# Local attention with a convolution branch: where the softmax inverse is applied, and which engine does three of the conv taps

## The chip, the cores and the metric

One core of a Trainium2 chip. The time is device microseconds of one execution; several executions are measured and the median is given. A profile of one further execution gives every instruction with its engine, start and duration. The engines are TensorE (PE; its weight loads are listed apart as PEld), VectorE (DVE), ScalarE (ACT), GpSimd (POOL) and the queue that issues most transfers, SyncE (SP).

## The reference

Three layers in float32 on a tensor of 2 images, 256 channels, 48 by 48 pixels. Only the first is touched by the change; after it come a state-space layer and a mixture of eight experts.

The first layer normalises the image by groups of channels and then computes two things from the normalised image `x`:

```python
q = (c1x1(x, Wq, bq) * HD ** -0.5)            # 4 heads of 64 channels
k, v = c1x1(x, Wk, bk), c1x1(x, Wv, bv)
att = softmax(einsum(q, unfold7x7(k) + unfold7x7(pe)))   # 49 neighbours of each pixel, reflected edges
out_att = einsum(att, unfold7x7(v))
hid = relu(dwconv3x3(x, w1))                   # one filter per channel
oc = dwconv3x3(hid, w2)
wts = softmax(einsum(Wfc, x), over 9)          # oc is the same for the nine, so the weights add up to 1
return rate1 * out_att + rate2 * oc            # added to the layer's input
```

## The kernel before

The first layer, called layer 0 here, is a *flow*: every piece of work is declared as an operation with an engine, a cost in ns, the operations it needs, the buffers it takes and frees, and a due time. Before anything is built, a planner (`Flow.run`) plays the flow through with these costs and writes out a fixed order for each engine; each engine then runs its list strictly in that order and waits at every instruction for what it needs. Due times are a block's number times `PACE0`, shifted by a table `LEAD0` with one entry for each kind of operation. So a cost or a lead that is edited changes the order on all engines. The GpSimd list is in order as well (`on_pool`): compute and the issue of transfers share it.

**Attention.** Each image is cut into 18 blocks of 8 by 16 queries, 36 blocks in all. A block sees 14 by 22 = 308 keys. The 256 channels lie as two halves (`h`) of 128 partitions, with two heads (`j`) in each half. For a block and a half, the steps are:

- `score` (L776, PE): two matmuls with 64 rows each, into a PSUM pair `banks`;
- `least` (L786, DVE): adds the mask, takes the minimum, writes `prob`;
- `exps` (L797, ACT): two exponentials over 308 keys, with the sums into `den`;
- once for the block, after both halves: `rden` (L852, DVE), the reciprocal of the four sums;
- `divide` (L803, ACT): two multiplications of 128x308 by the reciprocal;
- `turn` (L810, PE): six transposes of `prob`, keys onto the partitions, in chunks of 110, 110 and 88 keys (`KCH`);
- `copy` (L818, L819, ACT): two copies out of PSUM into `pt`;
- `mix` (L828, PE): six matmuls with the values `val` into a PSUM `bank`;
- `add` (L835, DVE): adds the product and the bias `bv1` onto the image.

The matmuls of `score` use half of the array's rows and those of `mix` half of its columns; the planner books a switch between these modes. Keys (L665, added with a place term at L671 and mirrored at the edges by `kb`, small copies on GpSimd, L678 to L685; the place term itself is made at L654), queries (L621, scaled at L631 in three pieces) and values (L711) are matmuls of their own. Values go through HBM into a table, and each block loads its part (L860) on the SP queue.

**Convolution.** Channels and rows are cut into 8 strips (two images, two halves, two strips of 24 rows). The first conv writes `hid`: the centre tap on ACT (L557), six taps on DVE (L561, multiply and add), and taps 1 and 7 by `added`: ACT multiplies into a tile `ct` (L599, two buffers), and a transfer issued on GpSimd adds the tile onto `hid` in SBUF (L603). Then relu on ACT (L565), and the second conv adds all nine taps onto the image on DVE (L573).

PSUM has room for four `bank` and two `banks` (pairs). After layer 0 the state-space layer starts with transposes of the image (L988), which need its last `add`.

Of the kernel before, what the change touches and what calls it, by code (L numbers as in the profile page):

```python
# [37 lines left out]
P = 128  # L38
# [3 lines left out]
HD = 64  # L42
# [5 lines left out]
KCH = ((0, 5), (5, 5), (10, 4))  # L48
# [74 lines left out]
class Flow:  # L123
# [8 lines left out]
    def __init__(self, room, lead):  # L132

        self.room, self.lead, self.ops = dict(room), lead, {}
# [8 lines left out]
    @classmethod  # L143
    def kind(cls, key):
        return key if isinstance(key, str) else cls.kind(key[0])

# [3 lines left out]
    def rank(self):  # L150

        after = {k: [] for k in self.ops}
        for k, o in self.ops.items():
            for n in o["needs"]:
                after[n].append(k)
        tail, left = {}, {k: len(after[k]) for k in self.ops}
        ends = [k for k in self.ops if not left[k]]
        for k in ends:
            o = self.ops[k]
            same = [tail[a] for a in after[k] if self.ops[a]["due"] == o["due"]]  # L160
            tail[k] = self.span(o) + max(same, default=0) + self.HOP
            for n in o["needs"]:
                left[n] -= 1
                if not left[n]:
                    ends.append(n)
        return {k: o["due"] - tail[k] - self.lead.get(self.kind(k), 0) for k, o in self.ops.items()}, after
# [62 lines left out]
class Kernel:  # L229
# [49 lines left out]
    def begin_flow(self, pool, room, pace, lead):  # L279

        self.m, self.pace, self.flow, self.tiles, self.last = pool, pace, Flow(room, lead), {}, {}
# [52 lines left out]
    def layer0(self, ctx):  # L334
# [5 lines left out]
        room = dict(bank=4, banks=2, q=2, prob=3, pt=4, val=3, vout=2, hid=2, place=2, ct=2)  # L340
        self.begin_flow(self.pool("att", 1, ctx), room, self.PACE0, self.LEAD0)
        self.kp = [wts.tile([P, HP, HP], F32, name=f"kp{h}") for h in range(NH)]
        self.xp = {(b, h): wts.tile([P, H, W], F32, name=f"xp{b}{h}") for b in range(B) for h in range(NH)}
# [19 lines left out]
    def prepare(self, wts):  # L363
# [15 lines left out]
        for key, cost in (("cst", 9500), ("vec", 9000), ("wp", 8500), ("Wk", 9500), ("Wq", 10500), ("Wv", 11500),  # L379
                          ("win", 22000)):  # L380
            self.arrival((key, 0), cost)
# [7 lines left out]
            new("w2r", NH * 9), v["w2"], r["rate2"], None, ALU.mult), ("vec", 0))  # L389

        self.op(0, ("bv1", 0), "DVE", 220, lambda: vec.tensor_scalar(
            new("bv1", NH), v["bv"], r["rate1"], None, ALU.mult), ("vec", 0))
        self.op(0, ("wv1", 0), "POOL", 1600, lambda: nc.gpsimd.tensor_scalar(
            l0["Wv"], l0["Wv"], r["rate1"], None, ALU.mult), ("vec", 0), ("Wv", 0))
# [63 lines left out]
    def group_norm(self, b):  # L458
# [7 lines left out]
        for h in range(NH):  # L466
# [7 lines left out]
            for i in range(pieces):  # L474
                if i % 2 == 0:
                    self.arrival(("x", (b, h, i // 2)), (4500, 16000)[b] + (i // 2 * NH + h + 1) * 700)
# [50 lines left out]
    def convolutions(self, b):  # L527
# [16 lines left out]
        for n in range(NH * strips):  # L544
# [33 lines left out]
            for k in (1, 7):  # L578
                last = self.added(due, ("1", key, k), rows[0], partial(tap, rows, k=k), hidden, lambda h=h: (self.xp[b, h], 0),
                                  lambda w=w1, k=k: w[:, k : k + 1], before, last)  # L580
            for k in range(9):
                if k != 4 and k not in (1, 7):
# [4 lines left out]
            rest = taps  # L587
            for i, k in enumerate(rest):
                self.op(due, ("c2", (key, k)), "DVE", 1385, partial(mac2, k), *before, uses=[("hid", key)] if i == len(rest) - 1 else [])
                before = [("c2", (key, k))]  # L590

    def added(self, due, key, first, places, out, of, weight, before, last):
# [3 lines left out]
        def product():  # L596
            t = self.large_tile("ct", key, [P, CR + 1, W])
            dst, src = places(o=(t, first), i=of())
            nc.scalar.activation(dst, src, AF.Identity, scale=weight())  # L599

        def issue():
            (dst, _), (t, _) = (places(o=o, i=of()) for o in (out(), (T["ct", key], first)))
            nc.gpsimd.dma_start(dst.rearrange("p r c -> p (r c)"), t.rearrange("p r c -> p (r c)"), accum_op=ALU.add)  # L603

        self.op(due, ("cp", key), "ACT", 1220, product, *before, takes=[("ct", key)])
# [4 lines left out]
    def queries(self, b, rb):  # L610
# [4 lines left out]
        for h in range(NH):  # L615
# [10 lines left out]
            def scale(h=h, key=key):  # L626
                if h == 0:
                    self.large_tile("q", (b, rb), [P, NH, NCB, QR * QC])
                ps = T["bank", ("q", key)][:, : QR * W].rearrange("p (r c) -> p r c", r=QR)
                for cb in range(NCB):  # L630
                    nc.scalar.activation(  # L631
                        T["q", (b, rb)][:, h, cb, :].rearrange("p (r c) -> p r c", r=QR), ps[:, :, cb * QC : (cb + 1) * QC],
                        AF.Identity, bias=l0["bq8"][:, h : h + 1], scale=-(HD ** -0.5),
                    )
# [3 lines left out]
            self.op(c, ("q", key), "ACT", 870, scale, ("qp", key), ("bq8", 0), ("q", (b, rb, 0)) if h else None,  # L638
                    takes=[] if h else [("q", (b, rb))], uses=[("bank", ("q", key))])

    def keys(self, b, g):
# [17 lines left out]
        for h in range(NH):  # L659
# [16 lines left out]
            def border(kp=kp):  # L676
# [4 lines left out]
                for j in range(PAD):  # L681
# [8 lines left out]
                    *[("score", (i, h)) for i in range(old + 1) if b],  # L690
# [64 lines left out]
    def block(self, c):  # L755
# [11 lines left out]
        for h in range(NH):  # L767
            key = (c, h)

            def scores(h=h, key=key):  # L770
                if h == 0:
                    self.large_tile("prob", c, [P, 4, NKEY])
                ps = self.banks_for(("s", key))
                for j in range(2):
# [4 lines left out]
                    )  # L779

# [20 lines left out]
            def divide(h=h):  # L801
                for a in range(2 * h, 2 * h + 2):
                    nc.scalar.mul(T["prob", c][:, a, :], T["prob", c][:, a, :], T["rden", c][:, a : a + 1])  # L803


            def turn(h=h, key=key):
                ps = self.banks_for(("t", key))
                for i, (kr, nr) in enumerate(KCH):
                    for j in range(2):
                        nc.tensor.transpose(  # L810
                            ps[: nr * KC, j, i * P : (i + 1) * P], T["prob", c][:, 2 * h + j, kr * KC : (kr + nr) * KC],
                            self.ident
                        )

            def copy(h=h, key=key):
                full, short = KCH[0][1] * KC, KCH[-1][1] * KC
                pt, ps = self.large_tile("pt", key, [P, 2, len(KCH), P]), T["banks", ("t", key)]
                nc.scalar.copy(pt[:full, :, :2, :].rearrange("p j i q -> p j (i q)"), ps[:full, :, : 2 * P])  # L818
                nc.scalar.copy(pt[:short, :, 2, :], ps[:short, :, 2 * P : 3 * P])  # L819


            def mix(h=h, key=key):
                po = self.bank_for(("o", key))
                for i, (kr, nr) in enumerate(KCH):
                    nk = nr * KC
                    for j in range(2):
                        a = 2 * h + j
                        nc.tensor.matmul(  # L828
                            po[j * HD : (j + 1) * HD, :P], lhsT=T["val", c][:nk, i, a * HD : (a + 1) * HD],
                            rhs=T["pt", key][:nk, j, i, :], start=i == 0, stop=i == len(KCH) - 1,  # L830
                        )

            def add(h=h, key=key):
                x = self.x[b][:, h, :].rearrange("p (r c) -> p r c", r=H)[:, r0 : r0 + QR, c0 : c0 + QC]
                nc.vector.scalar_tensor_tensor(  # L835
                    x, T["bank", ("o", key)][:, :P].rearrange("p (r c) -> p r c", r=QR), self.l0["bv1"][:, h : h + 1],
                    x, ALU.add, ALU.add
                )

            self.op(c, ("score", key), "PE", 512, scores, ("q", (b, rb, h)), *[k for k in rows if k[1][2] == h],  # L840
                    ("score", (c, 0)) if h else None,
                    takes=[("banks", ("s", key))] + ([] if h else [("prob", c)]), mode="rows", uses=[("q", (b, rb))] if last and h == NH - 1 else [])
            self.op(c, ("least", key), "DVE", 950, least, ("score", key), ("cst", 0), ("least", (c, 0)) if h else None,
                    uses=[("banks", ("s", key))])
            self.op(c, ("exps", key), "ACT", 1170, exps, ("least", key), ("exps", (c, 0)) if h else None)
            self.op(c, ("divide", key), "ACT", 990, divide, ("rden", c))
            self.op(c, ("turn", key), "PE", 655, turn, ("divide", key), takes=[("banks", ("t", key))], uses=[("prob", c)])
            self.op(c, ("copy", key), "ACT", 870, copy, ("turn", key), takes=[("pt", key)], uses=[("banks", ("t", key))])
            self.op(c, ("mix", key), "PE", 660, mix, ("copy", key), ("val", c), takes=[("bank", ("o", key))], mode="tiled",
                    uses=[("pt", key)] + ([("val", c)] if h == NH - 1 else []))  # L850
            self.op(c, ("add", key), "DVE", 350, add, ("mix", key), ("bv1", 0), uses=[("bank", ("o", key))])
        self.op(c, ("rden", c), "DVE", 175, lambda: nc.vector.reciprocal(self.small_tile("rden", c, wide), T["den", c]),  # L852
                *[("exps", (c, h)) for h in range(NH)])


        def load():
            val = self.large_tile("val", c, [P, len(KCH), C])
            for i, (kr, nr) in enumerate(KCH):
                nk, first = nr * KC, (r0 + kr) * KC
# [8 lines left out]
        "Wk": -1147950, "Wq": 130187, "Wv": -311640, "add": -66396, "bkp": -1659163, "bq8":  # L868
        487296, "bv1": -67420, "c1": 131452, "c2": -74690, "ca": -343085, "cd": 295831, "copy":
        828342, "cp": -194702, "cst": 1126755, "divide": 116227, "exps": -352759, "ga": 195685,  # L870
        "gneg": 849100, "gs": -87647, "ka": -73324, "kb": -515860, "kk": -132952, "least":
        512500, "line": 1189336, "mix": -72068, "place": -761695, "q": -313065, "qp": -156027,
        "rden": 1012714, "relu": 395339, "rstd": 172645, "score": 733004, "sw": -31974, "turn":
# [1491 lines left out]
```

## Time and profile before

| | |
|---|---|
| median of 4 runs | 1276.02 us (1274.98 to 1279.85) |
| the profiled execution | 1275.89 us, of which 1274.1 us lie between the first and the last instruction |
| mean granted TensorE clock | 0.983 |
| layer 0 in the profile | up to 309.3 us |
| all that follows | 964.8 us |
| busy over the whole span | PE 95%, DVE 72%, ACT 64%, POOL 45% |

The parts of the profile that are used: the page's busy times; a table of stages, which gives each engine's busy time in a stretch and the granted clock there; the groups of instructions, by line, with busy time, mean duration and what ended the idle time before them; the waits; and the timeline, instruction by instruction. A matmul's end is modelled, so for TensorE the distance from one start to the next start says more than the duration.

### The profile page before, as it was taken

How to read it: one execution, taken by the hardware profiler on the slowest of the kernel's cores; microseconds unless marked ns; L12 is line 12 of the kernel's file. 1: busy time of each engine (PE TensorE's matmuls, PEld its weight loads, DVE VectorE, ACT ScalarE, POOL GpSimd, SP SyncE). 2: the span in 40 equal slices, each digit the busy share in tenths (PEclk: the TensorE clock that was granted, in tenths of full speed). 3: DMA queues.
4: the chain of work that ended last, by engine and by line, in shares of the span. 5: the costliest groups of instructions: out<-in, count | busy, mean ns of one | idle time of the engine just before them, and what ended most of it. 6: DMA issues, size and time to landing. Idle time of an engine off the chain costs nothing. (4 is left out here: it accounts for less than half of the span.)

```text
span 1274.1 us, 23413 instructions
## 1 busy us (share of the span) xinstructions
PE 1211.7 (95%) x7952; PEld 966.0 (76%) x7952; DVE 911.6 (72%) x2401; ACT 815.7 (64%) x1978; POOL 574.3 (45%) x781
## 2 busy tenths in 40 slices
PE   4999899996999999999999999999999999999995
PEld 2666566655667777777776888999999999999994
DVE  6999789998587988889798655655555655556442
ACT  3999889998889988789697643333333333334342
POOL 4723503112267789899899873121212122212220
PEclk9999889999899999999999999999999999999998
DMA  8553527251223334334545149667657667656756
GB/s 280 147 147 99 136 90 175 77 128 31 74 77 95 100 115 121 120 107 142 169 148 175 55 135 290 186 230 227 221 173 258 184 229 221 229 174 218 224 178 211
DMA packets 103961, 203.74 MB, mean 160 GB/s; under 512 B 10891, under 2 KB 82908, under 8 KB 98908
## 3 DMA queue, kind: packets, MB, share of 16 engines
q1 hardware_dynamic: 85020, 168.51, 38.7%
q0 software_dynamic: 16704, 29.37, 12.1%
q10 hardware_dynamic: 2116, 4.33, 1.0%
q8 instruction: 65, 1.06, 0.3%
q14 instruction: 56, 0.46, 0.1%
HBM read 154.24 MB, written 43.23 MB: 155 GB/s over the span
## 5 line engine op out<-in xcount | busy, mean ns | idle before, releaser
L2094 POOL DMA_INDIRECT acc<-ey,token x70 | 108.9, 1555 | 369.8 <-ACT ey L2093 325.4
L2088 ACT ACTIVATE hid<-bank,bt 128x256 f32<-128x256 f32 (+1 forms) x288 | 132.3, 461 | 170.7 <-PE bank L2084 166.5
L2084 PE MATMUL bank<-ext,wt 128*128 128x256 f32 (+1 forms) x1152 | 241.2, 368 | 0.0
L2084 PEld LDWEIGHTS bank<-ext,wt 128*128 128x128 f32 x1152 | 207.0, 190 | 25.0
L573 DVE SCALAR_TENSOR_TENSOR x<-hid,w2r,x 128x1128 f32<-128x1128 f32 (+3 forms) x72 | 99.5, 1391 | 4.6 <-ACT hid L565 3.9
L2127 PE MATMUL po<-ts,ss 128*128 128x128 f32 x768 | 96.2, 275 | 0.0
L915 PE MATMUL bank<-xn,win 128*128 128x387 f32 x240 | 92.6, 509 | 2.1 <-ACT t L998 2.1
L1128 DVE SCALAR_TENSOR_TENSOR xc<-bank,vec,xc 128x384 f32<-128x384 f32 x144 | 86.6, 609 | 8.5 <-ACT xc L1117 8.1
L2127 PEld LDWEIGHTS po<-ts,ss 128*128 128x128 f32 x768 | 90.9, 192 | 0.0
L1344 ACT ACTIVATE mt<-mt,cum 128x128 f32<-128x128 f32 x288 | 87.7, 392 | 0.0
L2131 ACT COPY u<-po 128x128 f32<-128x128 f32 x32 | 8.5, 266 | 114.2 <-PE po L2127 114.2
L1678 POOL DMA_INDIRECT xs<-u,rows x72 | 73.3, 1018 | 17.5 <-issue 14.6
L797 ACT ACTIVATE prob<-prob,top 128x308 f32<-128x308 f32 x144 | 79.1, 570 | 0.4 <-DVE top L786 0.4
L2071 DVE TENSOR_TENSOR ss<-hid 128x512 f32<-128x512 f32 x32 | 22.1, 691 | 70.6 <-ACT hid L2088 70.6
L915 PE MATMUL zbank<-xn,win 128*128 128x384 f32 x192 | 71.5, 494 | 0.0
L1450 PE MATMUL bank<-wout,y 128*128 128x264 f32 x288 | 70.3, 389 | 0.1
L786 DVE CUSTOM_DVE_ANT_0 prob<-banks,cst 128x308 f32<-128x308 f32 x144 | 62.0, 471 | 11.1 <-PE banks L776 10.8
L810 PE MATMUL banks<-cst,prob 128*110 128x128 f32 (+1 forms) x432 | 61.9, 285 | 8.4 <-ACT pt L819 4.0
L803 ACT ACTIVATE prob<-prob,rden 128x308 f32<-128x308 f32 x144 | 68.9, 567 | 1.3 <-DVE rden L852 1.2
L810 PEld LDWEIGHTS banks<-cst,prob 128*110 128x110 f32 (+1 forms) x432 | 48.2, 133 | 28.0 <-issue 7.1
L561 DVE SCALAR_TENSOR_TENSOR hid<-xp,vec,hid 128x1175 f32<-128x1175 f32 (+1 forms) x48 | 69.2, 1443 | 0.1
L603 POOL DMA_DIRECT2D hid<-ct x16 | 14.1, 883 | 119.5 <-ACT hid L557 91.7
(333 smaller groups left out, 3000.9 us busy)
## 6 DMA issues: line engine op xcount, KB each, us to landing
wt<-in_We SPq DMA_DIRECT2D x36, 2048.0 KB
mt<-decays SPq DMA_DIRECT2D x36, 512.0 KB
ex<-xs SPq DMA_DIRECT2D x36, 265.0 KB
rd<-decays SPq DMA_DIRECT2D x68, 128.0 KB
val<-vtab SPq DMA_DIRECT2D x72, 110.0 KB
bt<-in_We SPq DMA_DIRECT2D x36, 136.0 KB
hid<-ct POOLq DMA_DIRECT2D x8, 600.0 KB, 5.5
hid<-ct POOLq DMA_DIRECT2D x8, 576.0 KB, 5.4
```

Source lines behind the costliest of these rows:

```text
L573: nc.vector.scalar_tensor_tensor(dst, src, w[:, k : k + 1], dst, ALU.mult, ALU.add)
L797: nc.scalar.activation(t, t, AF.Exp, bias=T["top", c][:, a : a + 1], scale=-1.0, accum_out=T["den", c][:, a : a + 1])
L810: nc.tensor.transpose(ps[: nr * KC, j, i * P : (i + 1) * P], T["prob", c][:, 2 * h + j, kr * KC : (kr + nr) * KC], self.ident)
L915: self.nc.tensor.matmul(ps, lhsT=lhs(k), rhs=rhs(k), start=k == 0, stop=k == NH - 1)
L1128: nc.vector.scalar_tensor_tensor(out(), T["bank", ("cv", at)][:, i : i + TB], wc[:, i : i + 1], out(), ALU.mult, ALU.add)
L1344: nc.scalar.activation(t, t, AF.Relu, bias=at_s, scale=-1.0)
L1450: nc.tensor.matmul(ps[:, : C + E], lhsT=T["y", c][:, m, :], rhs=self.l1["wout"][:, m, :], start=m == 0, stop=m == NZ - 1,)
L1678: ins = nc.gpsimd.indirect_dma_start(self.xs, bass.IndirectOffsetOnAxis(ap=of("rows")[:, i, q : q + 1], axis=0), T["u2", g][:, i, :], None,)
L2084: nc.tensor.matmul(ps[:, :rows], lhsT=w1[:, k, c * P : (c + 1) * P], rhs=xt[:, k, :], start=k == 0, stop=k == NH - 1,)
L2088: nc.scalar.activation(hid[:, c, :], ps[:, :rows], AF.Gelu, bias=bt[:, c : c + 1])
L2094: put = nc.gpsimd.indirect_dma_start(self.acc, bass.IndirectOffsetOnAxis(ap=token[:, j : j + 1], axis=0), y, None, compute_op=ALU.add)
L2127: nc.tensor.matmul(p[name], lhsT=v[a][:, c], rhs=v[w][:, c], start=c == 0, stop=c == NHC // 2 - 1)
```

## The change

All of it is in layer 0. The lists of all engines after layer 0 hold the same instructions in the same order as before.

- `divide` is gone. `turn` now follows `exps` and moves the exponentials as they are. The inverse sums are spread instead: GpSimd widens the block's four inverses to 128x256 (`rx`, L888 in the new file), two transposes on TensorE turn that (`rt`, L893), ScalarE copies it out of PSUM (`rc`, L899, into `rb`), and VectorE multiplies the value product by it (`norm`, L881, into `ot`) and adds it to the image (`add`, L877). These are one operation for a block, not one for a half.
- `score` (L810) and `mix` (L867) are one operation for a block. `mix` needs `rt`.
- The chunks of keys are 84, 112 and 112, always transposed 112 wide, so `copy` (L851) is one instruction for a half.
- Queries are scaled by one instruction (L667) in place of three.
- Second conv: the centre tap becomes a scaled copy with the bias on ACT into a new tile `cg` (L597); taps 1 and 7 go through `added` (L626, L638) onto `cg`; VectorE does six taps (L577) and one sum of `cg` onto the image (L603).
- PSUM: two `bank` and three `banks`. `LEAD0` has new values, one for each image; some booked arrival times are new. Small tiles of the later layers get a pool of their own.

```diff
-KCH = ((0, 5), (5, 5), (10, 4))
+KW = 112
+KCH = ((0, NKEY - 2 * KW), (NKEY - 2 * KW, KW), (NKEY - KW, KW))
...
-        room = dict(bank=4, banks=2, q=2, prob=3, pt=4, val=3, vout=2, hid=2, place=2, ct=2)
+        room = dict(bank=2, banks=3, q=2, prob=3, pt=4, val=3, vout=2, hid=2, place=2, ct=2, cg=2, rb=2, ot=1, rx=2)
...
+            def centre(h=h, top=top, key=key, hidden=hidden):
+                g = self.large_tile("cg", key, [P, CR, W])
+                dst, src = tap((top, top + CR), (g, top), hidden(), 4)
+                nc.scalar.activation(
+                    dst, src, AF.Identity, bias=self.l0["bv1"][:, h : h + 1],
+                    scale=self.l0["w2r"][:, 9 * h + 4 : 9 * h + 5]
+                )
+            def gather(key=key, strip=strip):
+                nc.vector.tensor_add(strip(), strip(), T["cg", key])
...
-            def divide(h=h):
-                for a in range(2 * h, 2 * h + 2):
-                    nc.scalar.mul(T["prob", c][:, a, :], T["prob", c][:, a, :], T["rden", c][:, a : a + 1])
...
-                nc.scalar.copy(pt[:full, :, :2, :].rearrange("p j i q -> p j (i q)"), ps[:full, :, : 2 * P])
-                nc.scalar.copy(pt[:short, :, 2, :], ps[:short, :, 2 * P : 3 * P])
+                nc.scalar.copy(pt[:KW].rearrange("p j i q -> p j (i q)"), ps[:KW, :, : len(KCH) * P])
...
+        self.op(c, ("mix", c), "PE", 1320, mix, *[("copy", (c, h)) for h in range(NH)], ("val", c), ("rt", c),
+                mode="tiled", uses=[*[("pt", (c, h)) for h in range(NH)], ("val", c)])
+        def scale():
+            po = T["bank", ("o", c)][:, : NH * P].rearrange("p (h q) -> p h q", h=NH)
+            nc.vector.tensor_tensor(self.large_tile("ot", c, [P, NH, P]), po, T["rb", c], ALU.mult)
...
+        def widen():
+            t = self.large_tile("rx", c, [P, 2 * NH, HD])
+            nc.gpsimd.tensor_copy(t, bcast(T["rden", c], 2, [P, 2 * NH, HD]))
+        def spread():
+            ps = self.bank_for(("o", c))
+            for h in range(NH):
+                nc.tensor.transpose(
+                    ps[:, (NH + h) * P : (NH + h + 1) * P], T["rx", c][:, 2 * h : 2 * h + 2, :].rearrange("p a d -> p (a d)"), self.ident
+                )
+        self.op(c, ("rx", c), "POOL", 1400, widen, ("rden", c), takes=[("rx", c)])
+        self.op(c, ("rt", c), "PE", 220, spread, ("rx", c), takes=[("bank", ("o", c))], uses=[("rx", c)])
```

## The prediction

> **What bounds the kernel now.** First the page's busy times, to see which engines can matter:
>
> ```profile
> PE 1211.7 (95%) x7952; PEld 966.0 (76%) x7952; DVE 911.6 (72%) x2401; ACT 815.7 (64%) x1978; POOL 574.3 (45%) x781
> ```
>
> These mix stages, so next the table of stages (length, then busy time of PE, PEld, DVE, ACT and POOL, granted clock, DMA share):
>
> ```profile
> 100.00:120.00 20.00, 20.00 (x136) 14.15 (x136) 19.32 (x39) 19.30 (x52) 5.90 (x19) 1.00 0.25 77
> ...
> 152.60:166.30 13.70, 12.37 (x72) 8.95 (x74) 6.84 (x15) 8.87 (x23) 0.36 (x1) 0.50 0.32 71
> ...
> 220.00:240.00 20.00, 19.66 (x145) 13.51 (x144) 19.94 (x40) 19.94 (x53) 0.86 (x1) 1.00 0.42 105
> ...
> 309.30:1274.10 964.80, 934.13 (x6008) 783.47 (x6008) 634.78 (x1809) 545.43 (x1269) 485.29 (x593) 0.99 0.53 168
> ```
>
> In layer 0 three engines are full at once; added up from 16 to 310 us PE is busy for 277 us, DVE 270, ACT 269. What follows, 964.8 us, keeps its order, so it is carried over unchanged and only layer 0 can move. Third, TensorE's timeline, to see whether "busy" is real there:
>
> ```profile
> 198.15 0.88 PE L828 MATMUL bank<-pt,val 110*64 110x128 f32 x12
> 198.96 0.80 PE L776 MATMUL banks<-kp,q 64*128 64x308 f32 x4
> 199.68 0.86 PE L810 MATMUL banks<-cst,prob 128*110 128x128 f32 x6
> 200.48 1.54 PE L828 MATMUL bank<-pt,val 110*64 110x128 f32 x24
> 201.95 1.32 PE L776 MATMUL banks<-kp,q 64*128 64x308 f32 x8
> 203.20 0.88 PE L828 MATMUL bank<-pt,val 110*64 110x128 f32 x12
> ...
> 149.40 0.80 PE L776 MATMUL banks<-kp,q 64*128 64x308 f32 x4
> 153.93 1.53 PE L810 MATMUL banks<-cst,prob 128*110 128x128 f32 x6 [3.73 <-ACT pt L819]
> ```
>
> It is real: each group starts where the one before it ends, and a group's price is the distance of starts. Only in places does TensorE wait, as at 149.4 us, for a copy on ScalarE. So TensorE is the first bound, and the other two engines cost only where they make it wait. Last, the groups that change:
>
> ```profile
> L573 DVE SCALAR_TENSOR_TENSOR x<-hid,w2r,x 128x1128 f32<-128x1128 f32 (+3 forms) x72 | 99.5, 1391 | 4.6 <-ACT hid L565 3.9
> L803 ACT ACTIVATE prob<-prob,rden 128x308 f32<-128x308 f32 x144 | 68.9, 567 | 1.3 <-DVE rden L852 1.2
> L828 PE MATMUL bank<-pt,val 110*64 110x128 f32 (+1 forms) x864 | 63.9, 288 | 3.6 <-ACT pt L818 1.7 <-DVE x L835 1.3 <-ACT vout L718 0.4
> L810 PE MATMUL banks<-cst,prob 128*110 128x128 f32 (+1 forms) x432 | 61.9, 285 | 8.4 <-ACT pt L819 4.0 <-DVE top L786 2.3 <-DVE rden L852 1.3
> L603 POOL DMA_DIRECT2D hid<-ct x16 | 14.1, 883 | 119.5 <-ACT hid L557 91.7 <-DMA hid<-ct 20.2 <-ACT ct L599 4.6
> ```
>
> **The change, part by part.** *ScalarE.* Divide goes: 68.9 us. The two copies of a half were 594 and 389 ns, so 205 ns more for 256 elements more; one of 768 elements is 800 ns: 72 x (983 - 800) = 13 less. Queries: 72 scalings with 21.1 us busy become 24 of 128x384, 490 to 665 ns each by the rows L1246 and L1117, 14 us: 7 less. Added: 36 `rc` by L998's 387 ns (same shape) is 14; 16 conv products by L599's 1282 ns, 20.5; 8 centre taps by L557's 1300 ns, 10.4. Sum: 44 us less, ACT falls from 269 to 225 us and is no longer full.
>
> *VectorE.* 24 taps of 1391 ns go (33.4). 8 sums of `cg` come, by L1352's 1211 ns for 1024 elements 1.36 us each (10.9). The 72 adds (L835, 23.7 us) give way to 36 `norm` and 36 `add` of 256 elements, by L1419's 413 ns 29.7. Net 16.5 less: 270 to 253.
>
> *TensorE.* By the starts above a lone score half costs 0.72 us and two together 1.25; a lone mix half 0.81, two 1.47. In the order before, 56 of 72 score halves stand alone, and 51 of 72 mix halves; after, none. Saved: 28 x 0.19 = 5.3 and 26 x 0.15 = 3.9. Twelve transposes in a row take 1.41 us (196.74 to 198.15), so the 72 of `rt` cost 72 x 0.118 = 8.5; if each pair forced two switches of mode, 0.15 each by the mix row, it would be 19. In the new order 15 of the 36 stand between operations of other modes, where I expect no extra switch for most. Sum about -1 us (from -3 to +10). So TensorE's own work stays, and a gain can come only from its waits.
>
> *TensorE's waits.* The rows L810 and L828 list 12.0 us of idle before PE. Beside it is the half clock. After the wait of 3.73 us the stage row shows 13.7 us at 0.50, which costs 6.85; 3.4 us at 268.7 had 0.50 as well, 1.7. Together 20.5 us. Most of it is named ACT (`pt` L818, L819, `vout`) or the inverse (`rden`), which the change relieves or takes off that path: `turn` no longer waits for both halves' sums and the division. The part that stays: VectorE's `top`, the start, and the wait for a `ct` buffer. The stall at 149.4 us itself came from that: L599 on ACT sat 4.11 us until a transfer had landed, with the copies behind it. The change has twice as many such products on the same two buffers, now with 44 us of spare time on ACT as the only cover. I take 12 of the 20.5.
>
> The Trainium skill ("TensorE: Matmul & The Clock Gate", section "What's actually happening") has full clock come back after about 3.4 us of busy time; this trace's stall took 13.7 us. By the page such a stall would cost 1.7 us in place of 6.85; the sum goes by the row.
>
> *GpSimd.* 36 `rx` of 128x256 have no row of their shape. Bounds: 0.25 us (L931, memset of 768 elements in 0.75, per element) and 1.34 (L449, 128x256, multiplied, under contention). Nearest is L449 undisturbed, 0.92 us at 59.8 us: 33 us in all, plus 16 issues of 883 ns, 14 us. GpSimd has room for that, but it meets VectorE:
>
> ```profile
> 90.10 0.99 POOL L654 TENSOR_TENSOR place<-line 128x480 f32<-128x480 f32 x1 [0.44 <-DVE kp L671]
> ...
> 133.19 2.07 POOL L654 TENSOR_TENSOR place<-line 128x480 f32<-128x480 f32 x1 [3.49 <-DVE kp L671]
> ```
>
> The same instruction takes 0.99 us where it starts first, and the conv tap that began 0.06 us after it then took 2.15 us (mean 1.39); it takes 2.07 where a tap was running. So each `rx` either waits up to a tap (1.4 us) or holds one back for up to 0.92. Multiply-adds of the conv fill 136 of VectorE's 253 us, so of 36 `rx` some 19 meet one: up to 18 us on VectorE, which eats the 16.5 saved. That is bearable while TensorE is the bound: VectorE would be at 253 to 271 of some 283 us.
>
> The Trainium skill ("SBUF — State Buffer", section "Who interferes with whom") gives the lock to any VectorE instruction with two inputs in SBUF against a GpSimd instruction that reads SBUF. By it the new `add` and the sums of `cg` are in it too, which no row here shows; another 26 us of VectorE would count, and 4 more `rx` would collide.
>
> *Late `rx`.* TensorE's list is in order, and `rt` stands in it ahead of `mix`; behind a late `rx` waits all of TensorE. Nothing in the trace shows this wait. Bounds: 0 (the planner books 1.4 us for `rx`, more than 0.92) and 36 x 1.4 = 50 us. I take 3 us, near the lower end, since `rx` is ready as early as `turn`, and turns and copies stand between.
>
> *PSUM.* Two `bank` in place of four, one of them held from `rt` to `norm`. Queries, keys and values take 62 banks for some 2.3 us each and blocks 36 for some 4: 287 of 2 x 290 us. No wait booked; bound 0 to 5 us.
>
> **Sum.** The profiled execution: 1275.9 - 1 - 12 + 3 = 1266 us; it lies 0.1 us under the median, so no correction.
>
> **The rivals.** *Slower: TensorE waits for `rx`.* GpSimd's list is in order too, and in the new one 18 of the 36 `rx` follow right on the issue of an accumulating transfer, which waits for the one before it to land: in the row of L603, 20.2 us over 5 waits, 4.0 each, out of 16 issues. With 32 issues that is 10 such waits, 5 or 6 of them ahead of an `rx`, 22 us. If half shows on TensorE, 11, with one half-clock stretch of 6.85, then 1276 - 13 + 18 = 1281; with a second, 1288. It decides from 13 us of new waits on. For it: these waits, and copies of `kb` that take 1.3 in place of 0.2 us under a tap, while the planner books 0.17. Against it: the slack ahead of `rt`.
>
> *No change: VectorE becomes the bound.* If the collisions cost the full 18 us and the new sums collide as well, VectorE needs 272 us and hardly ever waits; the gain is what TensorE's half clock gives less what VectorE adds: 1273 to 1278. Against it: VectorE waits for TensorE today (L786 has 11 us idle for `banks`).
>
> *More: all waits go.* 1276 - 3 - 20.5 gives 1252.
>
> **How the numbers follow.** Forecast (1254 to 1272): 0.53; all waits go: 0.07; no change: 0.12; slower: 0.28. A measurement of this kernel tells 0.3%, 3.8 us, from no change. So faster 0.60, same 0.12, slower 0.28. The range, 1250 to 1288, runs from the best case with a drain 2 us shorter to the slower rival with two half-clock stretches; outside are about 0.15.
>
> **What would show it.** Right: the first transposes after layer 0 (now 309.3 us) near 299; no stretch at half clock near 150 us; idle before the turns no longer named `pt`; ACT 225 us and DVE 253 to 271 in the stage. Wrong: PE's waits name `rx` on POOL for over 13 us, or a stall behind a `ct` product recurs, or VectorE's taps average over 1.5 us with VectorE never idle.

## The result and the profile after

The changed kernel takes 1279.49 us, median of 45 runs (1275.35 to 1287.27); the kernel before took 1276.40 us in the 71 runs beside it. The ratio is 1.003, interval 1.0021 to 1.0039: slower by 3.8 us by this ratio (the medians lie 3.1 apart), where 10 us less was forecast. The profiled execution has a span of 1278.9 us. Engine totals first, from the page after:

```profile
PE 1207.5 (94%) x8024; PEld 976.2 (76%) x8024; DVE 894.6 (70%) x2385; ACT 780.1 (61%) x1774; POOL 624.2 (49%) x833
```

Against the same line of before, the work moved as meant: TensorE 4.2 us less, VectorE 17.0 less, ScalarE 35.6 less, GpSimd 49.9 more. Three engines do less and the kernel is slower. Next the table of stages after (length; busy time of PE, PEld, DVE, ACT and POOL, each with its number of instructions; granted clock; DMA share and GB/s):

```profile
16.00:313.16 297.16, 271.20 (x2008) 190.75 (x2009) 251.93 (x555) 232.94 (x502) 135.35 (x231) 0.97 0.63 155
...
40.00:51.20 11.20, 8.06 (x31) 3.66 (x29) 10.35 (x24) 0.73 (x1) 8.45 (x20) 1.00 0.58 152
51.20:58.00 6.80, 4.65 (x12) 3.28 (x14) 1.30 (x4) 5.49 (x17) 3.70 (x10) 0.50 0.87 169
...
95.50:98.90 3.40, 3.40 (x11) 1.40 (x10) 1.08 (x6) 3.40 (x12) 0.00 (x0) 0.50 0.79 214
194.50:201.30 6.80, 5.81 (x35) 3.97 (x35) 2.17 (x4) 1.53 (x2) 1.95 (x6) 0.50 0.57 125
...
313.16:1278.90 965.74, 934.00 (x6008) 783.47 (x6008) 634.81 (x1808) 545.42 (x1269) 485.69 (x593) 0.98 0.53 168
```

The last row is the rest of the kernel: 965.7 us, 964.8 before. So the difference lies in layer 0. From its first key matmul to the first transposes of the next stage it takes 293.9 us (19.25 to 313.16), 289.9 before (19.39 to 309.30). The rows with 0.50 are stretches at half clock: the one near 150 us is gone, as foreseen, but there are three new ones, in all 17.0 us, as long as the two before. In the row from 40 us ScalarE is busy for 0.73 us of 11.20.

To part work from waiting, take TensorE between these two points: it is busy for 275.3 us before and 271.2 after, and idle for 14.6 and 22.7. So its own work fell by 4.1 us, the half clock stayed, and the idle time rose by 8.1. The table of waits names the holders after, from 30 to 300 us (us in total, times, the longest):

```profile
PE bank L748 <- ACT q L667: 5.3, 1, 5.3
PE banks L845 <- ACT pt L851: 3.9, 4, 1.9
PE bank L867 <- ACT rb L899: 3.3, 3, 1.4
PE bank L893 <- POOL rx L888: 3.1, 1, 3.1
PE bank L659 <- ACT vout L755: 3.0, 1, 3.0
```

Three of them are single waits of over 3 us, and a half-clock stretch of the table above begins within or just after each. Together they are 11.4 us; none of them has a counterpart before, where the one single wait of over 3 us was the 3.73 for `pt`, now gone. Each is traced back in the timeline (start, duration, engine, what; in brackets the idle time and its releaser). The first:

```profile
39.71 1.35 POOL L717 COPY kp<-kp 128x10 f32<-128x10 f32 x1
41.57 1.96 POOL L691 TENSOR_TENSOR place<-line 128x384 f32<-128x384 f32 x1
43.48 1.36 POOL L715 COPY kp<-kp 128x10 f32<-128x10 f32 x1
...
45.45 1.07 POOL L638 DMA_DIRECT2D hid<-ct  x1
...
50.47 1.29 ACT L626 ACTIVATE ct<-xp,vec 128x1200 f32<-128x1200 f32 x1 [10.50 <-DMA hid<-ct]
...
53.35 2.08 PE L748 MATMUL bank<-Wv,xp 128*128 128x256 f32 x4 [5.30 <-ACT q L667]
```

Read backwards: TensorE waits for a scaling of queries on ScalarE, which stands in ScalarE's list behind a `ct` product; that one waits 10.50 us until the first transfer has left a `ct` buffer. The transfer was issued at 45.45 because GpSimd's list before it was late: edge copies `kb` (L715, L717) of ten elements a partition take 1.35 us where a conv tap runs on VectorE, 0.19 to 0.22 elsewhere, and `place` takes 1.96. The copies were as slow in the kernel before (47.6 us busy on their two lines, 46.7 after); what is new is what stands behind them. This is the stall of 149.4 us over again, in another place. The second:

```profile
77.10 3.10 SPq L768 DMA_DIRECT2D vtab<-vraster  x2
80.25 4.43 SPq L774 DMA_DIRECT2D vtab<-vraster  x3
81.98 0.58 ACT L755 COPY vout<-bank 128x512 f32<-128x512 f32 x1
84.78 3.95 SPq L910 DMA_DIRECT2D val<-vtab  x6
88.84 5.96 SPq L758 DMA_DIRECT2D vraster<-vout  x3
93.83 0.59 ACT L755 COPY vout<-bank 128x512 f32<-128x512 f32 x1 [4.08 <-DMA vraster<-vout]
94.47 1.92 PE L659 MATMUL bank<-xp,Wq 128*128 128x384 f32 x4 [3.03 <-ACT vout L755]
```

A value copy made at 81.98 is stored by SyncE only from 88.84 on, since SyncE's own issues run late: the three of L774 take 4.43 us, where the same three took 1.85 before, and the two of L768 3.10 in place of 1.22. ScalarE then has no `vout` buffer, and the `bank` it should empty keeps TensorE waiting. Whether the four `bank` of before would have covered this wait or the first, no run tested. The third:

```profile
188.40 2.18 POOL L691 TENSOR_TENSOR place<-line 128x480 f32<-128x480 f32 x1 [4.04 <-DVE rden L883]
190.52 1.36 POOL L715 COPY kp<-kp 128x10 f32<-128x10 f32 x1
192.16 1.41 POOL L715 COPY kp<-kp 128x10 f32<-128x10 f32 x1
193.51 1.32 POOL L717 COPY kp<-kp 128x10 f32<-128x10 f32 x1
195.03 0.41 POOL L888 COPY rx<-rden 128x256 f32<-128x256 f32 x1
195.49 0.69 PE L893 MATMUL bank<-cst,rx 128*128 128x128 f32 x2 [3.08 <-POOL rx L888]
```

Here `rx` itself is quick, but it stands behind `place` and `kb`, which wait out taps one after the other. Last, the groups of instructions that the change made (busy us, mean ns, idle before them):

```profile
L565 DVE SCALAR_TENSOR_TENSOR hid<-xp,vec,hid 128x1175 f32<-128x1175 f32 (+1 forms) x48 | 69.5, 1452 | 1.0 <-DMA hid<-ct 1.0
L577 DVE SCALAR_TENSOR_TENSOR x<-hid,w2r,x 128x1128 f32<-128x1128 f32 (+1 forms) x48 | 66.0, 1382 | 0.1
L851 ACT COPY pt<-banks 112x768 f32<-112x768 f32 x72 | 54.9, 804 | 6.3 <-PE banks L845 6.1
L845 PE MATMUL banks<-cst,prob 128*112 128x128 f32 x432 | 57.7, 276 | 6.1 <-ACT pt L851 3.9 <-ACT prob L837 2.0
L867 PE MATMUL bank<-pt,val 112*64 112x128 f32 (+1 forms) x864 | 56.6, 280 | 3.3 <-ACT rb L899 3.3
L888 POOL COPY rx<-rden 128x256 f32<-128x256 f32 x36 | 36.3, 1008 | 73.4 <-DVE rden L883 63.7 <-PE bank L893 9.5
L626 ACT ACTIVATE ct<-xp,vec 128x1152 f32<-128x1152 f32 (+1 forms) x16 | 20.3, 1277 | 11.8 <-DMA hid<-ct 11.8
L626 ACT ACTIVATE ct<-hid,w2r 128x1104 f32<-128x1104 f32 (+1 forms) x16 | 19.5, 1239 | 1.5 <-DMA hid<-ct 0.8 <-DMA cg<-ct 0.7
```

### The profile page after: what moved, and what is told of

It is laid out like the page before. It is cut to its first block, busy times and chain, and to the rows that moved or that the text cites. A ratio compares the mean times of both kernels' runs of the same rounds, so it can differ in the third digit from the quotient of the medians.

```text
span 1278.9 us, 23472 instructions
## 1 busy us (share of the span) xinstructions
PE 1207.5 (94%) x8024; PEld 976.2 (76%) x8024; DVE 894.6 (70%) x2385; ACT 780.1 (61%) x1774; POOL 624.2 (49%) x833
## 5 line engine op out<-in xcount | busy, mean ns | idle before, releaser
L1737 POOL DMA_INDIRECT xs<-u,rows x72 | 73.0, 1014 | 17.5 <-issue 15.0
L888 POOL COPY rx<-rden 128x256 f32<-128x256 f32 x36 | 36.3, 1008 | 73.4 <-DVE rden L883 63.7
L577 DVE SCALAR_TENSOR_TENSOR x<-hid,w2r,x 128x1128 f32<-128x1128 f32 (+1 forms) x48 | 66.0, 1382 | 0.1
L2186 PE MATMUL po<-wt,hid 128*128 128x128 f32 x496 | 65.5, 275 | 0.0
L845 PE MATMUL banks<-cst,prob 128*112 128x128 f32 x432 | 57.7, 276 | 6.1 <-ACT pt L851 3.9
L974 PEld LDWEIGHTS bank<-xn,win 128*128 128x128 f32 x240 | 42.3, 194 | 24.6 <-issue 3.6
```

The lines of the kernel that those rows point to most:

```text
L577: nc.vector.scalar_tensor_tensor(dst, src, w[:, k : k + 1], dst, ALU.mult, ALU.add)
L974: self.nc.tensor.matmul(ps, lhsT=lhs(k), rhs=rhs(k), start=k == 0, stop=k == NH - 1)
L1737: ins = nc.gpsimd.indirect_dma_start(self.xs, bass.IndirectOffsetOnAxis(ap=of("rows")[:, i, q : q + 1], axis=0), T["u2", g][:, i, :], None,)
L2186: nc.tensor.matmul(p[name], lhsT=v[a][:, c], rhs=v[w][:, c], start=c == 0, stop=c == NHC // 2 - 1)
```

## The experiments

Theories: A, GpSimd's list is late because `kb` and `place` wait out taps, with transfers and `rx` queued behind; B, `rx` costs by itself, through its meetings with VectorE; C, the second conv's transfers crowd the buffers and the DMA queues; D, VectorE has no room. Ratios are against the kernel before in the runs beside it; layer 0 is read from one profile each, as above. What follows layer 0 keeps its order, and still it takes 964.6 to 975.0 us in these profiles (1011.0 in no_second_transfers). So whole spans of single profiles are not compared, and a gain in layer 0 counts where the ratio goes with it.

| run | layer 0, us | ratio (interval) |
|---|---|---|
| before | 289.9 | 1 |
| the change | 293.9 | 1.0030 (1.0021 to 1.0039) |
| kb_on_dve | 287.8 | 1.0009 (0.9995 to 1.0022) |
| before_kb_on_dve | 292.9 | 1.0046 (1.0031 to 1.0062) |
| rx_on_act | 291.8 | 1.0026 (1.0009 to 1.0042) |
| kb_on_dve_rx_on_act | 291.4 | 1.0021 (0.9998 to 1.0045) |
| no_second_transfers | 281.9 | not comparable |
| second_taps_on_dve | 302.4 | 1.0086 (1.0056 to 1.0117) |
| kb_and_second_taps_on_dve | 299.9 | 1.0060 (1.0032 to 1.0088) |
| attention_alone | 293.5 | 1.0048 (1.0026 to 1.0069) |
| third_vout | 288.7 | 1.0002 (0.9979 to 1.0026) |
| before_third_vout | 290.9 | 0.9995 (0.9974 to 1.0015) |
| kb_on_dve_third_vout | 284.4 | 0.9944 (0.9920 to 0.9969) |
| kb_priced | 285.6 | 0.9962 (0.9945 to 0.9978) |
| priced_kb_on_dve | 283.9 | 0.9953 (0.9931 to 0.9975) |
| priced_kb_on_dve_third_vout | 283.9 | 0.9927 (0.9901 to 0.9953) |

### Theory A: the edge copies

The edge copies go to VectorE, each at its place in the planned order, in the changed kernel and, as a control, in the kernel before:

```diff
-                    nc.gpsimd.tensor_copy(kp[:, rows, j : j + 1], kp[:, rows, 2 * PAD - j : 2 * PAD - j + 1])
+                    nc.vector.tensor_copy(kp[:, rows, j : j + 1], kp[:, rows, 2 * PAD - j : 2 * PAD - j + 1])
...
```

> The changed kernel with the edge copies of the keys (kb) put on VectorE in the place of the order where GpSimd had them; all else in the same order. Theory A, GpSimd's list runs late because these copies wait for conv taps, and the issue of the transfers and rx stand behind them: ScalarE's wait of 10.5 us for a ct buffer at 40 us shrinks to under 5, TensorE's wait for rx at 190 us (3.1 us) goes, and with them the half clock there; 1264 to 1270 us. Theory B, rx itself is the cost through its collisions with conv taps: 1276 to 1280 us, taps as long as now (1.45 us). Theory C, twice as many products share two ct buffers: the wait at 40 us stays at 8 us or more, 1275 to 1280 us.

> The kernel before with the edge copies of the keys on VectorE in the same place of the order. Theory A (GpSimd's list late): the same lateness exists there with less behind it; ScalarE's wait of 4.1 us for a ct buffer at 150 us goes, and the half clock after it; 12 to 20 us of VectorE's time are added where VectorE is full: 1265 to 1278 us. If VectorE is as tight as TensorE in the kernel before, it becomes slower, 1280 to 1290 us. Theories B and C say nothing on it.

In the changed kernel layer 0 falls by 6.1 us: TensorE's single waits for `q` and for `rx` are gone (ScalarE's wait for `ct` falls from 10.50 to 4.57 us), the half-clock stretches fall from 17.0 to 3.4 us, and the one long wait left is the value buffer near 90 us. By the ratios the step is 2.7 us (1.0030 to 1.0009), less than the one profile shows, and far from the 1264 to 1270 us that theory A gave. The same move makes the kernel before slower: ScalarE's wait for `ct` goes there too, but an inverse on VectorE (`rden`) now stands behind two sets of the moved copies, ScalarE waits 2.72 us for it at 145 us, and TensorE 3.1 us for the value copy that ScalarE has behind that. So the copies cost on VectorE (busy 266.1 us in layer 0 of the changed kernel against 251.9) and are worth moving only where a late GpSimd list stops TensorE, which is theory A; it isn't all, since the time stays level with before.

### Theory B: `rx` itself

```diff
-            nc.gpsimd.tensor_copy(t, bcast(T["rden", c], 2, [P, 2 * NH, HD]))
+            nc.scalar.copy(t, bcast(T["rden", c], 2, [P, 2 * NH, HD]))
```

> The changed kernel with rx made by ScalarE in the place of the order where GpSimd had it; all else in the same order. Theory A (GpSimd's list late): the wait for rx at 190 us goes, the one for a ct buffer at 40 us stays, since no rx stands ahead of it; 1272 to 1276 us. Theory B (rx itself): all collisions of rx with taps go, VectorE's taps fall from 1.45 to 1.40 us, 1262 to 1270 us. Theory C (ct buffers): 1277 to 1281 us.

> kb on VectorE and rx on ScalarE, same order: GpSimd keeps place, the transfers' issues and the weights' scalings. Theory A (rx was late only behind the kb copies): nothing more than kb_on_dve, 1276.5 to 1278.5 us, layer 0 287 to 289 us. Theory B (rx on GpSimd costs by its meetings with VectorE: mean 1008 ns against 394 ns undisturbed): VectorE's taps get shorter, 1.45 to 1.40 us, and the time falls by 3 us or more below kb_on_dve, 1274 us or less.

On ScalarE `rx` takes 410 ns in place of 1008 and waits for no tap. The stall near 190 us goes and layer 0 is 2.1 us shorter, yet the time stays that of the change (1.0026), with the stalls near 47 and 90 us where they were. VectorE's taps get no shorter to speak of (1408 ns against 1417). On top of kb_on_dve it brings nothing either; the layer was expected at 287 to 289 us and took 291.4, with a TensorE wait of 2.5 us near 90 us and one at half clock near 150; why it takes longer than kb_on_dve stays open. Theory B falls.

### Theories C and D: the second conv's products

no_second_transfers leaves out the 16 products and transfers of taps 1 and 7 of the second conv, so the image lacks them; the later stages change with it (1011 us in place of 966), and only layer 0 can be read. In second_taps_on_dve these taps are VectorE's again, in the places of their products:

```diff
+            if key[0] == "2":
+                b, h, _ = key[1]
+                x = self.x[b][:, h, :].rearrange("p (r c) -> p r c", r=H)[:, rows[0] : rows[1], :]
+                dst, src = places(o=(x, rows[0]), i=of())
+                nc.vector.scalar_tensor_tensor(dst, src, weight(), dst, ALU.mult, ALU.add)
+                return
             t = self.large_tile("ct", key, [P, CR + 1, W]) if dj == 1 else T["ct", key]
```

kb_and_second_taps_on_dve adds the move of `kb`. attention_alone declares the two taps as VectorE's in the flow, with the lead times searched anew:

```diff
-            rest = [k for k in taps if k not in (4, 1, 7)]
+            rest = [k for k in taps if k != 4]
...
-            for k in (4, 1, 7):
+            for k in ():
```

> The changed kernel without the 16 products and accumulating transfers of the second conv (taps 1 and 7 of it are left out of the result); all else in the same order. Theory C (twice as many products on two ct buffers): the waits of ScalarE for ct and the transfers' waits on GpSimd go, 1262 to 1270 us. Theory A (GpSimd's list late through the edge copies): the wait at 40 us belongs to the first conv and stays; 14 us less on GpSimd; 1274 to 1279 us. Theory B (rx itself): 1276 to 1280 us.

> The second convolution's taps 1 and 7 go back to VectorE as multiply-adds into x, at the place in the order where their products stood; their 16 products on ScalarE and 16 accumulating transfers go. Everything else keeps its order and every value is computed. VectorE gains 16 x 1.38 = 22 us (from about 249 to 271 us of busy time in layer 0), ScalarE loses 20. Theory C (the transfers cost time by crowding the DMA queues: SyncE's issues take twice as long under them, so a value store leaves 7 us late and ScalarE, then TensorE, wait for its buffer): TensorE's wait of 3.0 us near 91 us and its half clock go, the wait near 47 us (late kb copies on GpSimd) and the one named rx stay; layer 0 takes 282 to 286 us instead of 293.9, the time is 1268 to 1272 us. Rival D (VectorE has no room left, so taps put back on it delay least and the sums): layer 0 290 us or more, 1276 us or more, with TensorE's waits named prob L826 or rden.

> Both moves at once: the edge copies kb and the second convolution's taps 1 and 7 on VectorE, same order. VectorE about 275 us in layer 0. Theories A and C together (late GpSimd list and crowded queues are the two halves of what was lost): neither the wait near 47 us nor the one near 91 us is left, layer 0 277 to 282 us, 1263 to 1269 us. Rival D (VectorE as the bound): 288 us or more, as kb_on_dve or slower, 1277 us or more.

> The attention part and the one-copy halves with only the centre tap of the second convolution off VectorE (product with the bias on ScalarE and one sum); taps 1 and 7 are multiply-adds on VectorE, no second transfers; lead times searched anew for it. VectorE about 271 us of busy time, as the kernel before. Theory D (what the attention part frees on ScalarE is worth nothing while VectorE is as full as before): layer 0 287 to 293 us, ratio 0.998 to 1.003. Rival H (the attention part alone carries the gain, the transfers only spoil it): layer 0 278 to 284 us, ratio 0.991 to 0.996.

Without the products and transfers layer 0 takes 12.0 us less and the stall near 91 us is gone, while the first and the third stay (5.4 and 3.1 us of TensorE). ScalarE is busy for 17 us less there as well (215.6), so the 12.0 us need not be the transfers' alone. The queues show what goes with the stall. From 72 to 96 us in the changed kernel the accumulating transfers are 544 packets that fill 51.7% of the 16 DMA engines, beside 34.6% for the 2080 packets of the hardware queue; in second_taps_on_dve they fill 15.0% beside 44.1%, and SyncE's three issues take 1.86 us again in place of 4.43 (2.65 in no_second_transfers). Whether it is the kind of the transfers or the load as a whole that makes the issues long, these runs don't part.

But putting the taps back on VectorE costs far more than it frees. The table of stages of second_taps_on_dve:

```profile
16.00:322.16 306.16, 276.64 (x2009) 194.77 (x2009) 273.96 (x571) 216.65 (x486) 127.61 (x215) 0.94 0.46 121
```

VectorE goes from 251.9 to 274.0 us, layer 0 from 293.9 to 302.4, with five stretches of 6.8 us at half clock. It is as theory D had it: in this order VectorE's spare time was in use. An order of its own doesn't save it: attention_alone is slower than before as well, with VectorE at 269.5 us and the first stall (ScalarE 10.9 us on a `ct` buffer) still there. So in these orders the transfers carry more than they cost. Rival H, that the attention part alone gains, falls for the one order that the search found; it was searched with the old price of `kb`.

### The value buffer

A third buffer for `vout`, in its own ring; `wp` and `pos` move into a buffer that is taken later, to make room. Alone, in the kernel before, and with `kb` on VectorE:

```diff
+    RINGS, ring_at = {'vout': 3}, {}
...
+        if name in self.RINGS:
+            slot = self.ring_at[name] = (self.ring_at.get(name, -1) + 1) % self.RINGS[name]
...
-        wp = wts.tile([1, 2, P], F32, name="wp")
-        pos = wts.tile([1, 2, HP], F32, name="pos")
+        early = self.m.tile([P, CR, W], F32, tag="cg0", name="early")
+        wp = early.rearrange("p r c -> p (r c)")[:1, : 2 * P].rearrange("p (i c) -> p i c", i=2)
+        pos = early.rearrange("p r c -> p (r c)")[:1, 2 * P : 2 * P + 2 * HP].rearrange("p (i c) -> p i c", i=2)
```

> The changed kernel with a third buffer for the value copies and nothing else (kb stays on GpSimd, same order). Theory C, narrow: only the wait near 91 us goes (TensorE idle between 80 and 100 us 7.1 us in the changed kernel, 0.7 with kb on VectorE and a third buffer); the waits near 47 us (ct product behind the kb copies) and near 190 us (rx) stay. Layer 0 288 to 290 us instead of 293.9, 4 to 6 us less than the changed kernel, so about as the kernel before, ratio 0.998 to 1.0. Rival E (the wait only moves): layer 0 292 us or more, ratio 1.002 or more.

> The kernel before with a third buffer for the value copies (wp and pos kept in a hid buffer before its first use), same order: a control. In the kernel before no copy on ScalarE waits for a value buffer, since SyncE's stores leave at once. Theory C (the wait is made by the change's transfers): no difference, ratio 0.999 to 1.001, layer 0 289 to 291 us. Rival F (a third buffer helps any order): 3 to 5 us less, ratio 0.996 to 0.998.

> kb_on_dve with a third buffer for the value copies (vout; room is made by keeping wp and pos in a cg buffer before its first use), same order, all transfers kept. Theory C in its narrow form (the wait near 89 us is for a value buffer whose store SyncE issued late): ScalarE's wait at its vout copy, 4.67 us in kb_on_dve, goes, with TensorE's 3.7 us and the half clock of 3.4 us behind it; layer 0 282 to 284 us instead of 287.8, 1272 to 1274 us. Rival E (the values themselves arrive late, since the same store feeds the loads of val): the wait moves to mix a few us later, layer 0 287 us, 1277 to 1278 us.

All three come out as theory C has it, within half a us in layer 0. By the table of stages TensorE's idle time between 80 and 100 us falls from 5.2 us in the changed kernel to 1.0 in third_vout and 0.4 with `kb` moved too (the 7.1 and 0.7 of the expectation are too high by this view); in third_vout the other two stalls stay. The kernel before gains nothing: it had no such wait. With `kb` moved as well, the three single waits that the changed kernel had added are gone, and the kernel is 0.56% faster than before, 5.5 us in layer 0. Both moves together were not run in the kernel before; alone, one made it slower and the other left it level, and in before_kb_on_dve ScalarE waits for no value buffer, so the third would have nothing to take there. That speaks for a gain of the change itself, set free by the two moves.

### The planner's prices

Was the move needed, or only a right price? `kb` and `place` stay on GpSimd, at what the trace shows; the lead times are searched anew:

```diff
-        self.op(c, ("place", (b, g)), "POOL", 1100, place, ("line", 0), takes=[("place", (b, g))])
+        self.op(c, ("place", (b, g)), "POOL", 2000, place, ("line", 0), takes=[("place", (b, g))])
...
-            self.op(c, ("kb", key), "POOL", 6 * 170 + (3 * 180 if r0 == 0 or r1 == H else 0), border, ("ka", key),
+            self.op(c, ("kb", key), "POOL", 1200 + 6 * 170 + (3 * 180 if r0 == 0 or r1 == H else 0), border, ("ka", key),
```

> The changed kernel with two prices of its planner corrected to what the trace shows, kb 1.2 us dearer (its first copy waits out a tap) and place 2.0 instead of 1.1 us, and the lead times searched anew for these prices; kb, rx and all transfers stay on GpSimd, nothing is computed otherwise. Theory A (the list of GpSimd was late because kb was planned too cheap): no wait of ScalarE of over 5 us for a ct buffer and no TensorE wait of over 3 us named rx or q; layer 0 284 to 289 us, ratio 0.995 to 1.0. Rival G (GpSimd meets VectorE's taps wherever the copies are put, price or not): layer 0 292 us or more, ratio 1.002 or more.

0.9962 at 285.6 us: the instructions of the change, in another order, gain 4.9 us against before. A new search moves other things too, so not every us of the 8.3 between this and the change is the price's; but the stalls near 47 and 91 us are gone, as theory A said. The kernel before was planned with the same low prices, and no run searched it anew with the right ones. The third stall came back, against theory A's own condition, and shows that the price is still too low:

```profile
175.80 2.18 POOL L691 TENSOR_TENSOR place<-line 128x480 f32<-128x480 f32 x1 [2.96 <-DVE rden L883]
177.92 1.35 POOL L715 COPY kp<-kp 128x10 f32<-128x10 f32 x1
179.22 0.40 POOL L717 COPY kp<-kp 128x10 f32<-128x10 f32 x1
179.55 1.41 POOL L715 COPY kp<-kp 128x10 f32<-128x10 f32 x1
180.91 1.32 POOL L717 COPY kp<-kp 128x10 f32<-128x10 f32 x1
182.16 1.42 POOL L715 COPY kp<-kp 128x10 f32<-128x10 f32 x1
183.51 1.32 POOL L717 COPY kp<-kp 128x10 f32<-128x10 f32 x1
184.77 0.40 POOL L888 COPY rx<-rden 128x256 f32<-128x256 f32 x1
185.22 0.69 PE L893 MATMUL bank<-cst,rx 128*128 128x128 f32 x2 [3.22 <-POOL rx L888]
```

Five of the six copies of one `kb` waited out a tap each, not the first alone as priced. Two last kernels take the copies off GpSimd in this order, without and with the third value buffer; no other edit:

> kb_priced with the kb copies on VectorE, in kb_priced's order. Theory A: TensorE's wait of 3.7 us for rx at 181 us goes, with its half clock (10.2 us at 0.50, so 5.1 us): layer 0 276 to 279 us instead of 285.6, ratio 0.988 to 0.993. Rival D (VectorE, 250 of 286 us busy, pays for 23 us of small copies): layer 0 284 us or more, ratio 0.995 or more.

> The same with a third value buffer. In kb_priced ScalarE waited only 3.0 us for a value buffer in all, 1.6 us at most. Theory C: little left to take, layer 0 0 to 2 us less than priced_kb_on_dve, ratio 0.987 to 0.993. Rival D: 284 us or more, 0.995 or more.

The wait for `rx` and its half clock go, yet layer 0 falls by less than 2 us, to 283.9, not to 276 to 279. The table of stages of priced_kb_on_dve_third_vout suggests why:

```profile
16.00:302.55 286.55, 270.12 (x2009) 186.30 (x2009) 264.83 (x698) 233.28 (x502) 93.62 (x87) 1.00 0.66 161
```

Full clock, no TensorE wait of over 1.3 us after the first key matmul, and VectorE at 264.8 of 286.6 us, 11 more than in kb_priced (253.8). That the copies have eaten what the wait gave, as rival D said, is the likely reading; no run tests it by itself. TensorE is idle for 13.8 us still, in small pieces over all of the layer, against 14.6 in kb_priced. This version has the lowest ratio, 0.9927, but its interval overlaps those of the other three that gain.

## Why the prediction was wrong

The gain of 10 us did not come, and 3.8 us were lost. Step by step:

- **ScalarE** fell by 35.7 us (268.6 to 232.9) in layer 0, not by 44. The rows were right: `pt` 804 ns for 800, queries 13.9 us for 14, `rc` 13.4 for 14, products 19.5 for 20.5. But ScalarE starts an instruction before the last one has ended, so rows overlap: those of before add up to 328.6 us in 268.6 of busy time, those after to 277.3 in 232.9, and a sum of rows overstates what leaves the engine. TensorE was priced by starts, ScalarE wasn't. That the engine is no longer full was right.
- **VectorE**: 16.5 less forecast, 17.5 measured (269.4 to 251.9). The collisions, up to 18 us on VectorE, didn't show there: taps of over 1 us average 1409 ns before and 1417 after. GpSimd paid instead: `rx` 0.40 us free and 1.0 on the mean, with 20 of the 36 over 1.2 us where 19 were expected to meet a tap.
- **TensorE's own work**: 1 less forecast (3 less to 10 more), 4.1 less measured as busy time.
- **TensorE's waits, the failed step.** "I take 12 of the 20.5" counted which old waits the change relieves. In place of 12 us less, TensorE's idle time in layer 0 rose from 14.6 to 22.7 us, and the half clock stayed at 17.0 us in all. Of the 12.0 us of idle time before turns and mixes (rows L810 and L828 before), 9.4 are left (L845 and L867 after): `pt` is still named with 3.9 us, one wait of 1.9 near 150 us among them, and `rb`, which the change itself brings, with 3.3. So little was relieved, and the new order has tight places of its own, the three single waits of 5.3, 3.1 and 3.0 us; the stall behind a `ct` product, which the prediction named as a sign of being wrong, is the longest. Each term of what followed was in the prediction as a note and priced at little or nothing: the two `ct` buffers with "44 us of spare time on ACT as the only cover" (spare time on average is no cover at 40 us, where ScalarE had nothing else it was allowed to start); "copies of `kb` that take 1.3 in place of 0.2 us", put into a rival only; the two `bank`, "no wait booked", where TensorE waited 3.0 us for one to be emptied. The value stores that SyncE issues late were in no step: the transfers were priced at GpSimd's 14 us of issues, and not for what they do to the other queue.
- **Late `rx`**: 3 us taken, 3.1 measured, once, with 6.8 us at half clock behind it. That the sum has the right size here is luck, since nothing in the trace before showed the wait. The cause was `place` and `kb`, not the transfer issues that the slower rival counted; that rival had the sign by another mechanism.
- **Half clock**: the 13.7 us of the row were taken for a stall, against the 3.4 of the page; the runs lie between, see the last section. Of the 13.7, 1.3 lay within the wait, so the stall cost some 6.2 us and not 6.85, an estimate from half of the other 12.4.
- **What was right after all**: with the named waits removed the kernel is faster than before. The new order, the moved copies and the third buffer together have the ratio 0.9927, which puts the time of 1276.02 at 1266.7 us (1263.4 to 1270.0). Layer 0 of that profile gives 6.0 of the 9.3 us; for the rest one profile is too few.

What stays open is how much of kb_priced's gain is the price and how much the new search, what such a search would give the kernel before, and whether the 13.8 us of small waits can go.

## What to carry to other kernels

Where work has a fixed order on each engine, the waits of the old order say nothing of the waits of a new one: look in the new lists for the first place where an instruction stands behind one that can be late (a buffer on its second use, a transfer issue behind small copies, a store behind other issues), and price a single wait of over 3 us with its half clock. A planner's price must be the duration in company: copies of 0.2 us that cost 1.35 beside VectorE's taps stood in an order that looked better on paper and ran slower. Price a queue that overlaps its instructions by distances of starts, and a transfer by what it does to the other queues as well.

## What the runs showed of the hardware

- Stretches at half clock came in steps: 3.4, 6.8, 10.2 or 13.7 us. In the 16 profiles of this case there are 17 TensorE waits of 3 to 5.8 us in layer 0, and each has one, begun 2.1 us or more after the wait began and 6.2 us long on the mean. 5.1 us of it come after the wait's end, so some 2.6 us are lost beyond the wait, an estimate at half clock. The length doesn't follow from the wait: 3.73 us gave 13.7 in the kernel before, and 3.78 at the same place gave 6.8 in before_third_vout. Waits of 1.9 us were followed by 3.4 us in four profiles and by nothing in two. The Trainium skill ("TensorE: Matmul & The Clock Gate", section "What's actually happening") has the gate look at a free-running window of about 3.4 us, which fits the steps. It has full clock come back after one busy window or more; one window is here the shortest case (6 of the 17), not the usual one.
- Another engine's issues were slower while accumulating transfers filled the queues: SyncE's three issues took 4.43 us where these filled 51.7% of the DMA engines, 1.86 in second_taps_on_dve, where they filled 15.0%.
- A GpSimd copy of ten elements a partition took mostly 0.19 to 0.22 us, and 1.3 to 1.4 when it started while a conv tap, a multiply-add with two inputs in SBUF, had just begun on VectorE; the taps kept their length (1409 ns before, 1417 after). In the changed kernel 14 such copies ended 0.06 us after the tap that they had met. The Trainium skill ("SBUF — State Buffer", section "Who interferes with whom") has a VectorE instruction with two inputs in SBUF contend with a GpSimd instruction that reads SBUF, with the order of issue deciding which of them blocks; the durations agree with it.
